# A two-layer transformer on one core: the second attention's stores issued further behind their producers, and its fronts begun twelve steps sooner

## The chip, the cores and the metric

The kernel runs on one core of one Trainium2 chip. The metric is the device time of one execution in microseconds (us). The core has five engines, each with a queue of its own, filled in the order in which the program was written: TensorE (PE, its weight loads shown as PEld), VectorE (DVE), ScalarE (ACT), GpSimd (POOL) and SyncE (SP), whose queue issues most of the DMAs. An instruction that waits for another engine, or for a DMA, holds up what stands behind it in its own queue.

## The reference

`x` is 16 x 512 tokens of 128 numbers, 8192 tokens. Two blocks follow each other, and each adds an attention and a feed-forward network of the normed input to `x`:

```
xn = layernorm(x);  x = x + attn0(xn) + ffn0(xn)     # attn0: 4 layers of mamba, attention, mlp
xn = layernorm(x);  x = x + attn1(xn) + ffn1(xn)
```

The change touches the second block alone. `attn1` has 16 heads of 64. Queries and keys are rotated by position; keys serve as values too. A window of 128 queries sees its own and the previous window's keys, layer-normed, and one key for each 16 tokens that lie wholly before the query:

```
pkv = softmax(gkv @ Wproj)                  # over the 16 tokens of a segment
gkv = layernorm(sum of the 16 tokens, weighted by pkv)
sim = [q @ gkv (masked), q @ layernorm(local keys) (masked)]
out = softmax(sim) @ [gkv, layernorm(local keys)]
attn1 = out (all heads) @ Wout + bout
```

`ffn1` sends each token to the one of 8 experts that has its largest routing probability (at most 1024 tokens an expert), and adds the expert's output times that probability.

## The kernel before, in words

The first block fills some 5650 us and is not touched. The second block is written by a Python scheduler that runs when the program is built: `manual_schedule` keeps the instructions in exactly the order in which the Python code emits them, engine by engine.

The tokens are cut into 64 **units** of 128 (four to a sequence, `TB` = 4, `t` = 0 to 3 within it). Each unit has 16 heads in four **groups** of four heads. The main loop (from L1475) runs over 256 groups, `i` = 4 x unit + group. In a turn it emits

- `scores(i)` (L1327): four matmuls `s` into PSUM; four VectorE operations `am` that add the mask and take the maximum (L1350); four exponentials on ScalarE (L1351); a copy `pg` of the weights of the segment keys;
- `weights_by_key(i - 1, two)` for `two` = 0, 1 (L1359): transposes `gp` and `pp` on TensorE and copies `gt` (VectorE) and `pt` (ScalarE). The PSUM pool of `s`, `gp` and `pp` has five buffers, so `pp` of group i - 1 takes a buffer that `am` of group i has just read;
- `values(i - 2, two)` (L1378): matmuls `o` of the weights with `gvb` (segment keys) and `lk` (local keys), and for every second group a copy `ot` on ScalarE.

Between these the loop calls `work(1)`, six times a turn. `work` is one **cycle** of the rest: Python generators, called streams, each with the number of the cycle at which it may go on. A stream that yields `-n` lets n cycles pass; `+n` does the same and also ends the cycle for the streams after it in the list; 0 asks again in the next cycle. A unit's four turns take 24 cycles. The streams, in order of rank:

- `back(u)` (L1407), put in when the last scores of unit u are written: reciprocal of the sums, transposed into `rd`, `rd` stored to DRAM (L1418) and read back as `rb`, spread over the partitions (L1425); when the unit's values are written (`U.done`), GpSimd multiplies `ot` by `rb` (L1430); four cycles later TensorE's output projection `m_po` (eight matmuls, and `x1`), VectorE's bias addition `ro` (L1437) and, two cycles on, the store `r_d` (L1439).
- `front(u)` (L1157), the keys and queries of unit u: load `xu`; projections `m_kv`, rotated (`by_cos` on VectorE, copy `raw` on ScalarE, `raw`, `kv` on GpSimd); projections `m_q`, their products `q` on VectorE, their sum `qt` on GpSimd (L1208); mean `hm` and difference `hd` (VectorE), `by_w` (GpSimd, L1217), squares `hq` (ScalarE), `hv` and `pl` (VectorE, L1222 and L1234); `hr` and `hw`, the inverse root (ScalarE, GpSimd); transpose `m_plt`; normed keys `n`, segment softmax `se`; transposes `m_nt` into `lkt` (L1261); `lk` (L1271); `sw`, `m_gp`, `gm` to `gv` for the segment keys (`gr` L1296 to L1298, `lk` again L1299, `gv` L1304); `gv` stored to DRAM (L1308), transposed as `m_gkt`, and read back into `gvb` by four loads (L1323). `front(u)` starts only when front u - 1 has written `n` (`normed`).
- `routing()` (L999): the routing of all tokens, then 64 scatters of 128 tokens each to the experts' rows in DRAM (`xts` loaded by SyncE, L1079; indirect DMA on GpSimd, L1081), then the experts, 16 halves of 512 rows (`m_xep`, `m_hp`, `he`, `m_yp`, `ye`).
- `results()` (L1129): when all experts are written, for each tile of 128 tokens a gather `gy` (indirect DMA on GpSimd, L1137), a load `res` of the attention's result (L1144), three cycles, the sum `res` on VectorE (L1146) and at once the store to `out` (L1147).

Buffers that the change is near: `qt` has three, `lk` four (`lks[u % 4]`, read by units u and u + 1), `xts` four, `gv_d`, `rd_d` and the blocks `gvb` two each; the pool behind `misc`, for all PSUM of the streams, two.

The loop calls `begin()` for two fronts ahead of the first turn and then one at the first group of each unit; `while unfinished(i // 4): work(1)` holds the scores of a unit back until its front is written.

Of the kernel before, what the change touches and what calls it, by code (L numbers as in the profile page):

```python
# [23 lines left out]
NT = T // P  # L24
# [45 lines left out]
def tile_kernel(  # L70
# [16 lines left out]
    nc = tc.nc  # L87
# [38 lines left out]
    with (  # L126
# [770 lines left out]
        while done_t[0] < n_cycles or ready or streams or due or deferred:  # L897
            i, at = divmod(done_n[0], PC)
# [19 lines left out]
            if ready and ready[0][0] <= tick[0]:  # L918
                at, k, i = ready.pop(0)
# [3 lines left out]
            if do_t and done_t[0] % 4 == 3:  # L923
                k, t = divmod(done_t[0], 8)
# [14 lines left out]
    with (  # L939
# [59 lines left out]
        def routing():  # L999
# [73 lines left out]
            nc.vector.tensor_copy(slot, sl)  # L1073
            yield -1
            xts = {}
            for t in range(NT + 3):
                if t < NT:
                    xts[t] = wk.tile([P, D], F32, name=f"xts_{t}", tag="xts", bufs=4)
                    nc.sync.dma_start(xts[t], xt_d[t * P : (t + 1) * P, :])  # L1079
                if t >= 3:  # L1080
                    nc.gpsimd.indirect_dma_start(  # L1081
                        out=xe_d,
                        out_offset=bass.IndirectOffsetOnAxis(ap=slot[:, t - 3 : t - 2], axis=0),
                        in_=xts.pop(t - 3),
                        in_offset=None,
                    )
                yield -2
# [41 lines left out]
        def results():  # L1129

            while not experts_done[0]:
                yield 0
            for t in range(NT):
                while stored[0] <= t:
                    yield 0
                gy = wk.tile([P, D], F32, name=f"gy_{t}", tag="gy", bufs=3)
                nc.gpsimd.indirect_dma_start(  # L1137
                    out=gy,
                    out_offset=None,
                    in_=ye_d,  # L1140
                    in_offset=bass.IndirectOffsetOnAxis(ap=slot[:, t : t + 1], axis=0),
                )
                res = wk.tile([P, D], F32, name=f"res_{t}", tag="res", bufs=3)
                nc.sync.dma_start(res, r_d[t * P : (t + 1) * P, :])  # L1144
                yield -3
                nc.vector.scalar_tensor_tensor(res, gy, pk[:, t : t + 1], res, ALU.mult, ALU.add)  # L1146
                nc.sync.dma_start(out[t * P : (t + 1) * P, :], res)  # L1147

        class Unit:
# [7 lines left out]
        def front(u):  # L1157
# [30 lines left out]
            k, c_, s_ = halves(kv), halves(by_cos), halves(raw)  # L1188
            nc.gpsimd.tensor_tensor(k[:, :, 0, :], c_[:, :, 0, :], s_[:, :, 1, :], ALU.subtract)  # L1189
            nc.gpsimd.tensor_tensor(k[:, :, 1, :], c_[:, :, 1, :], s_[:, :, 0, :], ALU.add)  # L1190
            U.qt = wk.tile([P, NHP, P], F32, name=f"qt_{u}", tag="qt", bufs=3)
            for c in range(2):
                parts = []
# [53 lines left out]
            nc.vector.tensor_tensor(se, plv, smx.unsqueeze(2).broadcast_to(shape), ALU.subtract)  # L1247
            nc.scalar.activation(se, se, AF.Exp)
            U.normed = True
            yield 2  # L1250
            ss = wk.tile([H1, n_seg], F32, name=f"ss_{u}", tag="ss")
            nc.vector.tensor_reduce(ss, se, AX.X, ALU.add)
            nc.vector.reciprocal(ss, ss)
# [2 lines left out]
            for c in range(2):  # L1256
                ps = misc(f"nt_{u}_{c}")
                n2 = n.rearrange("p h d -> p (h d)")
                for i in range(4):
                    at = (4 * c + i) * P  # L1260
                    nc.tensor.transpose(ps[:, i * P : (i + 1) * P], n2[:, at : at + P], ident)  # L1261
                nc.scalar.activation(
                    lkts[b % 2][:, 4 * c : 4 * c + 4, t * KW : t * KW + P],
                    ps.rearrange("p (i t) -> p i t", t=P),
                    AF.Identity,
                    scale=g_col,
                    bias=b_col,
                )
                yield 1
            lk = U.lk  # L1270
            nc.gpsimd.tensor_tensor(lk, n, row(1).unsqueeze(1).broadcast_to(heads), ALU.mult)  # L1271
            ps = misc(f"pwp_{u}")
# [32 lines left out]
                gv, gd.unsqueeze(1).broadcast_to([P, 2, DH1]), row(4).unsqueeze(1).broadcast_to([P, 2, DH1]), ALU.add  # L1305
            )
            yield -5
            nc.sync.dma_start(gv_d[u % 2], gv[:, 0, :])  # L1308
            ps = misc(f"gkt_{u}")
            nc.tensor.transpose(ps[:, 0:P], gv.rearrange("p a d -> p (a d)"), ident)  # L1310
            for a in range(2):
# [5 lines left out]
                nc.scalar.copy(to, keys.unsqueeze(2).broadcast_to([64, NHP, n, n_seg]))  # L1317
            yield 1
            yield -2
            src = gv_d[u % 2].rearrange("(g j s) d -> j s g d", j=4, s=n_seg)  # L1320
            for j in range(4):
                at = 32 * j + t * n_seg
# [4 lines left out]
        def scores(i):  # L1327

            u, g = divmod(i, 4)
            U = units[u]  # L1330
            b, t = divmod(u, TB)
            n = NK if t else KW
            at = max(t - 1, 0) * KW
            if g == 0:
                U.done = False
                U.sum = wk.tile([P, H1], F32, name=f"sum_{u}", tag="sum", bufs=2)
            G = groups[i] = Group()
            G.pts = []
            pr = G.pr = wk.tile([P, 4, NK], F32, name=f"pr_{i}", tag="pr", bufs=2)
            pss = []  # L1340
            for j in range(4):
                h = 4 * g + j
                hp, r = h // 2, slice(64 * (h % 2), 64 * (h % 2) + 64)
                s = ps_s.tile([P, S], F32, name=f"s_{i}_{j}", tag="s")
                mm(s[:, 0:n], U.qt[r, hp, :], lkts[b % 2][r, hp, at : at + n])
                pss.append(s)
            for j, s in enumerate(pss):

                nmax = wk.tile([P, 1], F32, name=f"am_{i}_{j}", tag="am", bufs=8)
                nc.vector.tensor_tensor_reduce(pr[:, j, 0:n], s[:, 0:n], mask(t), -1.0, BIG, ALU.add, ALU.min, nmax)  # L1350
                nc.scalar.activation(  # L1351
                    pr[:, j, 0:n], pr[:, j, 0:n], AF.Exp, bias=nmax, scale=-1.0, accum_out=U.sum[:, 4 * g + j : 4 * g + j + 1]
                )
            G.pg = wk.tile([P, 4, NSEG], F32, name=f"pg_{i}", tag="pg", bufs=2)
            nc.scalar.copy(G.pg, pr[:, :, W:KW])
            if g == 3:
                streams.insert(0, [back(u), tick[0] + 2])

# [19 lines left out]
        def values(i, two):  # L1378
# [24 lines left out]
                U.ot = wk.tile([P, NHP, P], F32, name=f"ot_{u}", tag="ot", bufs=2)  # L1403
            nc.scalar.copy(U.ot[:, 2 * g - 2 : 2 * g + 2, :], U.o)
            U.done = g == 3

        def back(u):  # L1407

# [5 lines left out]
            nc.tensor.transpose(ps[0:H1, 0:P], U.sum, ident)  # L1414
            rd = wk.tile([H1, P], F32, name=f"rd_{u}", tag="rd", bufs=2)
            nc.vector.tensor_copy(rd, ps[0:H1, 0:P])
            yield 2
            nc.sync.dma_start(rd_d[u % 2], rd)  # L1418
            x1 = wk.tile([P, P], F32, name=f"x1u_{u}", tag="x1u", bufs=2)
            nc.sync.dma_start(x1, x1_d[b][:, t * P : (t + 1) * P])  # L1420
# [7 lines left out]
            yield -1  # L1428
            units.pop(u)
            nc.gpsimd.tensor_tensor(U.ot, U.ot, rb, ALU.mult)  # L1430
            yield -4
            po = misc(f"po_{u}")
            for i in range(NHP):
                mm(po[:, 0:D], U.ot[:, i, :], wout_sb[:, i, :], i == 0, False)
            mm(po[:, 0:D], x1, ident, False, True)
            res = wk.tile([P, D], F32, name=f"ro_{u}", tag="ro", bufs=2)
            nc.vector.tensor_tensor(res, po[:, 0:D], bout_row, ALU.add)  # L1437
            yield 2
            nc.sync.dma_start(r_d[u * P : (u + 1) * P, :], res)  # L1439
            stored[0] = u + 1  # L1440
            yield -1

        streams = []
        tick = [0]

        def work(n):

# [27 lines left out]
        begin()  # L1475
        NG1 = 4 * NU
        for i in range(NG1 + 2):
            if i % 4 == 0 and begun[0] < NU:
                begin()
            if i < NG1:  # L1480
                while unfinished(i // 4):
                    work(1)
                scores(i)
                work(1)
            for two in range(2):
                if 0 <= i - 1 < NG1:
                    weights_by_key(i - 1, two)
                    work(1)
                if i >= 2:
                    values(i - 2, two)  # L1490
                    work(1)
            work(1)
# [108 lines left out]
```

## Time and profile before

| | us |
|---|---|
| Median of 3 runs (7825.79 to 7835.86) | 7826.6 |
| Profiled execution's own time | 7828.71 |
| Its span | 7826.9 |
| First scores of unit 0 in the span | 5684.5 |
| TensorE busy over the span | 7010.5 (90%) |
| VectorE, ScalarE, GpSimd busy | 4782.5, 4616.3, 3012.6 |
| Mean granted TensorE clock | 0.938 |

In the rows of the profile, a line names the engine, the line of the kernel, the operation, the tile written and the tiles read, and in brackets or behind a bar the idle time ahead of it with the work that ended that idle time. A row of waits gives the waiting engine, line and tile, the releaser, the total, the number of times and the longest. `SPq` is SyncE's queue. Where matmuls go through the helper of the second block, their line is L994, so tiles tell them apart.

### The profile page before, as it was taken

The page shows a single profiled execution, that of the slowest core. Times are in us where ns is not written, and L with a number is a line of the kernel's source. Part 1 is how long each engine was busy: PE and PEld are TensorE (multiplying, and loading weights), DVE is VectorE, ACT ScalarE, POOL GpSimd, SP SyncE. Part 2 cuts the span into 40 slices and gives each one's busy share as a digit, 9 for nine tenths or more (in the row PEclk, how much of TensorE's full clock was granted, in tenths as well). Part 3 has the DMA queues.
Part 4 walks back from the last instruction along what each step waited for, and adds up shares of the span by engine and source line. Part 5 has one row for each costly group of instructions (what it writes and reads, how often), then busy time and mean ns, then how long its engine had stood idle before and what let it go on. Part 6 is the DMA issues. An engine that isn't in the chain of part 4 may idle for free. (4 is left out here: it accounts for less than half of the span.)

```text
span 7826.9 us, 107889 instructions
## 1 busy us (share of the span) xinstructions
PE 7010.5 (90%) x38168; PEld 3230.2 (41%) x38168; DVE 4782.5 (61%) x9622; ACT 4616.3 (59%) x9357; POOL 3012.6 (38%) x3763
## 2 busy tenths in 40 slices
PE   6898999999999999999999999999678999889898
PEld 2233333333333333333333333333256666666666
DVE  4565666566666666666666666666266555666665
ACT  3565655566555666656666666656355666556666
POOL 3333332232323233222222222222268655667775
PEclk7999999999999999999999999999789999989999
DMA  2221222212222221122211222222211111111111
GB/s 70 80 81 66 74 69 66 85 62 68 69 71 69 70 66 65 63 67 70 71 60 62 69 79 71 81 74 88 83 28 52 51 41 46 42 44 34 33 35 36
DMA packets 394780, 492.23 MB, mean 63 GB/s; under 512 B 82304, under 2 KB 278016, under 8 KB 393088
## 3 DMA queue, kind: packets, MB, share of 16 engines
q1 hardware_dynamic: 390144, 476.94, 19.5%
q0 software_dynamic: 4096, 8.40, 0.4%
q8 instruction: 302, 4.95, 0.3%
q14 instruction: 238, 1.95, 0.1%
HBM read 348.87 MB, written 133.17 MB: 62 GB/s over the span
## 5 line engine op out<-in xcount | busy, mean ns | idle before, releaser
L915 DVE TENSOR_REDUCE nm<-n 128x1 f32<-128x512 f32 x4096 | 2587.5, 682 | 1479.6 <-PE n L177 1477.9
L917 ACT ACTIVATE pt<-t 128x512 f32<-128x512 f32 x4096 | 2216.3, 595 | 1882.1 <-PE t L177 1857.4
L177 PE MATMUL n<-kt,qt 72*128 72x512 bf16 x4096 | 1323.5, 389 | 203.5 <-DVE nm L915 158.9
L177 PE MATMUL t<-qt,kt 75*128 75x512 bf16 x4096 | 1357.9, 391 | 104.1 <-ACT pt L917 56.0
L177 PE MATMUL o<-pt,vt 128*32 128x512 f32 x8192 | 1123.0, 671 | 0.0
L177 PEld LDWEIGHTS <-qt 72*128 72x128 bf16 x4096 | 354.7, 98 | 1026.3 <-issue 881.9
L177 PEld LDWEIGHTS <-kt 75*128 75x128 bf16 x4096 | 399.9, 99 | 849.8 <-issue 519.8
L1351 ACT ACTIVATE pr<-pr,am 128x288 f32<-128x288 f32 (+1 forms) x1024 | 508.0, 498 | 209.8 <-DVE am L1350 209.2
L867 POOL CAST nmp<-nm 128x16 bf16<-128x16 f32 x256 | 50.0, 195 | 1451.3 <-DVE nm L915 1451.3
L177 PEld LDWEIGHTS o<-pt,vt 128*32 128x32 f32 x8192 | 231.0, 118 | 661.1 <-issue 526.0
L467 POOL TENSOR_TENSOR qk<-qk,parts 128x512 f32<-128x512 f32 x128 | 147.9, 1155 | 769.3 <-ACT parts L280 739.7
L1350 DVE CUSTOM_DVE_ANT_0 pr<-s,cst 128x288 f32<-128x288 f32 (+1 forms) x1024 | 372.6, 419 | 44.5 <-PE s L994 44.1
L1373 PE MATMUL pp<-ident,pr 128*128 128x128 f32 x1792 | 311.5, 294 | 94.5 <-DVE am L1350 93.6
L994 PE MATMUL o<-pt,lk 128*64 128x128 f32 x3584 | 327.3, 300 | 0.0
L1375 ACT COPY pt<-pp 128x512 f32<-128x512 f32 (+1 forms) x512 | 264.9, 526 | 97.4 <-PE pp L1373 95.8
L1200 DVE TENSOR_TENSOR q<-m_q,cst 128x512 f32<-128x512 f32 x256 | 177.1, 692 | 220.1 <-PE m_q L994 220.1
L994 PE MATMUL s<-lkt,qt 64*128 64x288 f32 (+1 forms) x2048 | 298.3, 408 | 0.4 <-ACT lkt L1317 0.4
L177 PE MATMUL m_in<-x,w 128*128 128x512 f32 x512 | 279.6, 632 | 17.9 <-POOL x L330 9.7
L1373 PEld LDWEIGHTS pp<-ident,pr 128*128 128x128 f32 x1792 | 214.8, 148 | 162.9 <-DVE am L1350 130.2
L994 PE MATMUL m_q<-xu,wq_sb 128*128 128x128 f32 x2048 | 278.5, 279 | 1.9 <-ACT raw L1183 0.8
L177 PE MATMUL m_f<-n,w 128*128 128x512 f32 x512 | 274.0, 618 | 2.9 <-POOL n L330 2.6
L994 PEld LDWEIGHTS m_q<-xu,wq_sb 128*128 128x128 f32 x2048 | 249.4, 192 | 20.1 <-ACT raw L1183 16.0
(333 smaller groups left out, 11104.7 us busy)
## 6 DMA issues: line engine op xcount, KB each, us to landing
qt<-q_d SPq DMA_DIRECT2D x768, 96.0 KB
kt<-k_d SPq DMA_DIRECT2D x256, 288.0 KB
rb_n<-rstd_d SPq DMA_DIRECT2D x64, 512.0 KB
rb<-rd SPq DMA_DIRECT2D x128, 256.0 KB
q_d<-parts SPq DMA_DIRECT2D x64, 384.0 KB
k_d<-parts SPq DMA_DIRECT2D x64, 384.0 KB
o_d<-og SPq DMA_DIRECT2D x512, 36.0 KB
oa<-o_d SPq DMA_DIRECT2D x64, 256.0 KB
```

Source lines behind the costliest of these rows:

```text
L177: nc.tensor.matmul(out, lhsT=lhsT, rhs=rhs, start=first, stop=last)
L467: nc.gpsimd.tensor_tensor(x, x, parts[:, 0], ALU.subtract)
L867: nc.gpsimd.tensor_copy(parts[:, 0], nm)
L915: nc.vector.tensor_reduce(dst, n, AX.X, ALU.max, negate=True)
L917: nc.scalar.activation(dst, n, AF.Exp)
L994: nc.tensor.matmul(out, lhsT=lhsT, rhs=rhs, start=first, stop=last)
L1200: nc.vector.tensor_tensor(q, ps.rearrange("p (i t) -> p i t", t=P), const(name)[:, t * P : (t + 1) * P].unsqueeze(1).broadcast_to([P, 4, P ...
L1350: nc.vector.tensor_tensor_reduce(pr[:, j, 0:n], s[:, 0:n], mask(t), -1.0, BIG, ALU.add, ALU.min, nmax)
L1351: nc.scalar.activation(pr[:, j, 0:n], pr[:, j, 0:n], AF.Exp, bias=nmax, scale=-1.0, accum_out=U.sum[:, 4 * g + j : 4 * g + j + 1])
L1373: nc.tensor.transpose(pp[:, a, c, :], G.pr[:, 2 * two + a, at : at + P], ident)
L1375: nc.scalar.copy(pt[:, :, 0:n, :], pp[:, :, 0:n, :])
```

## The change

Nothing is computed differently. The order in which instructions are written, and so the order in each queue, changes:

- `routing()`: the scatter of a tile is written two steps behind its load, no longer three.
- `results()`: four cycles pass between the sum `res` and its store to `out`.
- `front(u)`: two guards, `while scored[0] < u - 2` ahead of `qt` and `while valued[0] < u - 2` ahead of `lk`; `normed` is followed by three cycles, no longer two; the store of `gv` moves from ahead of `m_gkt` to three cycles behind it, and four cycles pass before the `gvb` loads.
- `back(u)`: `rd` is stored five cycles behind its copy (two before); `m_po` follows `ot` by six cycles (four before); `r_d` is stored five cycles behind `ro` (two before).
- `scored` counts the units whose last scores are written (set at the end of `scores`), `valued` those whose last values are (at the end of `values`).
- The main loop begins a front at the third group of a unit, twelve cycles sooner than at the first group of the next, and a third one at the very start.

```diff
-            for t in range(NT + 3):
+            for t in range(NT + 2):
...
-                if t >= 3:
+                if t >= 2:
                     nc.gpsimd.indirect_dma_start(
                         out=xe_d,
-                        out_offset=bass.IndirectOffsetOnAxis(ap=slot[:, t - 3 : t - 2], axis=0),
-                        in_=xts.pop(t - 3),
+                        out_offset=bass.IndirectOffsetOnAxis(ap=slot[:, t - 2 : t - 1], axis=0),
+                        in_=xts.pop(t - 2),
...
                 nc.vector.scalar_tensor_tensor(res, gy, pk[:, t : t + 1], res, ALU.mult, ALU.add)
+                yield -4
                 nc.sync.dma_start(out[t * P : (t + 1) * P, :], res)
...
             nc.gpsimd.tensor_tensor(k[:, :, 1, :], c_[:, :, 1, :], s_[:, :, 0, :], ALU.add)
+            while scored[0] < u - 2:
+                yield 0
             U.qt = wk.tile([P, NHP, P], F32, name=f"qt_{u}", tag="qt", bufs=3)
...
             U.normed = True
-            yield 2
+            yield 3
...
+            while valued[0] < u - 2:
+                yield 0
             lk = U.lk
...
             yield -5
-            nc.sync.dma_start(gv_d[u % 2], gv[:, 0, :])
             ps = misc(f"gkt_{u}")
...
             yield 1
             yield -2
+            nc.sync.dma_start(gv_d[u % 2], gv[:, 0, :])
+            yield -4
             src = gv_d[u % 2].rearrange("(g j s) d -> j s g d", j=4, s=n_seg)
...
+            scored[0] += g == 3
...
+            valued[0] += U.done
...
             nc.vector.tensor_copy(rd, ps[0:H1, 0:P])
-            yield 2
+            yield 5
             nc.sync.dma_start(rd_d[u % 2], rd)
...
             nc.gpsimd.tensor_tensor(U.ot, U.ot, rb, ALU.mult)
-            yield -4
+            yield -6
             po = misc(f"po_{u}")
...
             nc.vector.tensor_tensor(res, po[:, 0:D], bout_row, ALU.add)
-            yield 2
+            yield 5
             nc.sync.dma_start(r_d[u * P : (u + 1) * P, :], res)
...
+        scored, valued = [0], [0]
...
-            if i % 4 == 0 and begun[0] < NU:
+            if (i == 0 or i % 4 == 2) and begun[0] < NU:
                 begin()
```

## The prediction

> **What bounds the kernel now.** I read the table of stretches first, to see what the second attention costs, then who waits on TensorE there, then one unit's rows on TensorE, VectorE and GpSimd, last the stalls of SyncE's queue. I call one step of the written schedule a cycle; a unit has 24. The stage's units start where the `s` rows start (eight matmul rows a group, four groups a unit).
>
> ```profile
> 5804.20:6136.30 332.10, 279.35 (x2349) 207.53 (x2348) 204.18 (x591) 196.39 (x585) 270.72 (x253) 0.94 0.19 52
> 6136.30:6680.80 544.50, 513.73 (x4187) 375.47 (x4186) 311.16 (x900) 335.10 (x945) 309.22 (x285) 0.99 0.17 44
> 6680.80:7040.40 359.60, 293.52 (x2353) 219.98 (x2352) 221.28 (x630) 193.47 (x582) 237.95 (x227) 0.89 0.17 44
> 7040.40:7706.30 665.90, 598.27 (x5175) 448.64 (x5174) 445.11 (x1321) 428.07 (x1278) 477.63 (x440) 0.96 0.13 34
> ```
>
> Columns: stretch, length, busy us of PE, PEld, DVE, ACT, POOL, granted clock. These are units 3–12 (scatter beside them), 13–27 (experts), 28–37 (results caught up), 38–59 (nothing beside them): 33.2, 36.3, 36.0 and 30.3 us a unit. TensorE is busy 84 to 94%: its idle time and its clock are what can be won. Who makes it wait, from unit 0 on:
>
> ```profile
> PE pp L1373 <- DVE am L1350: 93.6, 48, 6.8
> PE m_po L994 <- POOL ot L1430: 66.7, 56, 3.8
> PE o L994 <- DMA gvb<-gv: 33.3, 8, 5.2
> PE m_nt L1261 <- DVE se L1247: 28.1, 23, 1.4
> ```
>
> The change aims at the last three. The first is the largest. A `pp` transpose of group i-1 needs the PSUM buffer that `am` of group i empties, so VectorE must reach `am` of a group soon after TensorE has made its scores, or TensorE stops. One late unit shows it:
>
> ```profile
> 7449.78 1.24 PE L994 MATMUL s<-lkt,qt 64*128 64x288 f32 x8
> 7453.83 2.05 PE L994 MATMUL m_po<-wout_sb,ot 128*128 128x128 f32 x16 [0.69 <-POOL ot L1430]
> 7456.85 1.24 PE L994 MATMUL s<-lkt,qt 64*128 64x288 f32 x8
> 7459.99 0.66 PE L1373 MATMUL pp<-ident,pr 128*128 128x128 f32 x4 [1.64 <-DVE am L1350]
> ```
>
> ```profile
> 7452.28 1.21 DVE L1211 TENSOR_REDUCE hm<-kv 128x16 f32<-128x1024 f32 x1
> 7453.53 1.33 DVE L1213 SCALAR_TENSOR_TENSOR hd<-hm,kv 128x1024 f32<-128x1024 f32 x1
> 7456.14 0.29 DVE L1437 TENSOR_TENSOR ro<-m_po,rows_sb 128x128 f32<-128x128 f32 x1 [1.28 <-PE m_po L994]
> 7456.35 1.21 DVE L1222 TENSOR_REDUCE hv<-hq 128x16 f32<-128x1024 f32 x1
> 7458.34 1.22 DVE L1234 TENSOR_REDUCE pl<-by_w 128x16 f32<-128x1024 f32 x1 [0.78 <-POOL by_w L1217]
> 7459.48 0.45 DVE L1350 CUSTOM_DVE_ANT_0 pr<-s,cst 128x288 f32<-128x288 f32 x1
> ```
>
> From the third group's scores to the released `pp` pass 10.2 us (7449.78 to 7459.99), and VectorE's norm chain sets them: `hm`, `hd`, ACT's `hq`, `hv`, `pl`. The 0.69 before `m_po` lies inside these 10.2 us, so it costs nothing there. In units 28–37 another wait decides:
>
> ```profile
> 6766.63 0.33 SPq L1308 DMA_DIRECT2D gv<-gv  x1
> 6776.17 0.34 SPq L1147 DMA_DIRECT2D out<-res  x1
> 6776.55 0.43 SPq L1144 DMA_DIRECT2D res<-r_d  x1
> 6777.10 1.34 SPq L1323 DMA_DIRECT2D gvb<-gv  x4
> ```
>
> ```profile
> 6779.03 0.76 PE L994 MATMUL o<-gt,gvb 128*128 128x128 f32 x2 [5.09 <-DMA gvb<-gv]
> ```
>
> SyncE's queue stands 9.5 us at the `out` store, behind a VectorE result, with the `gvb` loads queued after it.
>
> **The change part by part.** Line numbers are before's.
>
> Stores (`out` L1147, `r_d` L1439, `gv` L1308, `rd` L1418) leave SyncE's queue free. The four `gvb` loads then wait only for the values that read the old block. Issued most of a group ahead of the values that read the new block, they land in time: the 32.1 us of `gvb` waits in units 28–37, and the lower clock (0.89 against 0.96), go. `r_d` later by three cycles delays only `res`, which no engine but VectorE's `res` row waits for. `gv` later by three cycles lets `gvb` follow it by four. The later `rd` leaves some 6 cycles, about 7 us, for `rb` before `ot`; hidden behind two groups of values, and without that cover it would cost what the one `rb` wait of the trace cost, 13.2 us on GpSimd. As `out` now takes 7 cycles a tile instead of 3, results catch up at two a unit, and take units 31–59 instead of 28–37: GpSimd's `gy` gather (1.09 us) and VectorE's `res` (0.33) come twice in each.
>
> Scatter lag 3 to 2 (L1076): SyncE's 186.8 us of waits before `xts` loads shrink; TensorE waited for none of it. Cost 0; with its cover (loads four cycles ahead) gone, at most one landing a tile. The two guards (`scored`, `valued`): in the written order neither ever holds a front back. But GpSimd now writes `qt` and `lk` only 5 and 4 cycles (1.28 us each) behind TensorE's last reads of those buffers, before 15 and 14. TensorE needs under 2 us for such reads, and GpSimd stands idle 2.8 us ahead of `gr` anyway: cost 0, and some 2 us of GpSimd a unit if the cover is gone, ahead of `raw`, which is in the bounds below.
>
> `ot` to `m_po` two cycles wider: the 66.7 us go nearly everywhere, but only where that wait is not inside VectorE's chain does time go. `m_nt` one cycle wider: 12.1 us over 22 late units, 0.55 a unit, go.
>
> Fronts twelve steps sooner, with `po` later, change who shares a group, and this is the term that decides. Before, the norm chain shares its group with `m_po`. After, the written order of TensorE's heavy group is `s, gkt, gp, pp, q, o, pp, o, s`; `m_po` sits two groups later, beside `nt` and `gp`. VectorE's order is four `am`, `gt`, the last `q`, `hm`, `hd`, `hv`, `pl`, `res`, then the next `am`; GpSimd's is `qt, gy, by_w`, with `ot` gone from among them. From that group's scores: `am` starts at 0.8 and the four take 1.5; `q` ends on TensorE at 2.9, on VectorE at 3.6; `hm` 1.25, `hd` 1.35, `hq` 1.15, `hv` 1.2: 8.6. GpSimd: `gr` now stands behind four `am`, so `gv` ends and `raw` starts 2.2 us later after its group's scores than before (6.6 for 4.4), that is 2.1 before the heavy scores; `raw` 2.4, `kv` 2.4, `qt` 1.25 bring 4.0; the second `qt` 1.25 to 2.25, `gy` 1.25, `by_w` 2.35: 8.8 to 9.8. So `pl` starts there, ends at 10.0 to 11.0, `res` 0.3, `am` to `pp` 0.5: 10.8 to 11.9. Without `gy` and `res` 10.6. I take 11.4, nearest to the row of the second `qt`, which took 2.26 in every late unit beside `hd`: +1.2 (bounds +0.4, +1.7).
>
> The same shift moves 2.1 us of `m_po` (7453.83 to 7455.94) out of the stretch that VectorE sets, and a `q` (1.0) and `gkt` (0.2) into it: 1.0 us of TensorE work that was free must be paid elsewhere (+1.0; bounds +0.8, +1.1). `q`'s first product waits for the `raw` copy, now behind four exponentials: +0.4 (0, +0.7). TensorE's stop grows from 1.64 to about 5 us. After 1.64 us the second `pp` ran 1.06 instead of 0.66, after 5.09 `m_po` took 3.62 instead of 2.05. The granted clock over this late unit is 0.94, 3.7 us at half speed, 1.8 lost; over the 39.9 us of the unit with the 5.09 it is 0.87, 10.4 us at half, of which the stop itself covers some. One half-speed stretch more, partly under the stop: +0.7 (0, +1.7). With `m_nt` -0.5 (bounds -1.4, 0): **+2.8 us a late unit**, 33.1 us.
>
> [...]
>
> The sum, stretch by stretch:
> - units 38–59: 22 x 2.8 = +62, and +6 for two of the last four.
> - units 28–37: 36.0 to 33.1, -29.
> - experts, 13–27: the expert matmuls now fill the heavy group (5.1 us of its own, 3.3 of experts), so TensorE needs there what VectorE's chain needs without `gy`. `m_po` 14.7 and `m_plt` 9.3 us of waits go, `raw` and a small `pp` wait come: -0.7 x 15 = -10 (-1.9 to +1.0 each).
> - units 3–12: a scatter (1.02 us) stands where `gy` does, 33.1 for 33.2: 0 (-1.9 to +2.3 each).
> - start and tail: more of front 1 ahead of the first scores, +4 (-10, +15).
>
> Together +33. The profiled execution took 7828.7 us (span 7826.9), the median of the runs is 7826.6, 2.1 less. 7828.7 + 33 - 2.1 = 7860 us.
>
> **The rivals.**
> *Faster:* the chain ends no later than today (`by_w` in time, no `raw` wait, the same clock window). Then +1.2 a unit: 24 x 1.2 = 29, catch-up -45, scatter -17, experts -10, ends +4: -39, 7788 us. For it: `ot` leaves GpSimd's chain; against it: `gr` and `gy`. It decides below +2.1 a unit (44 units break even at 32.4 us).
> *Much slower:* the second `qt` is held through `hd` and `gy` follows late, two half-clock windows each unit: +4.2, 24 x 4.2 = 101, -15, +13, -5, +10: +104, 7930 us.
> *No effect:* SyncE's stops were mostly hidden (424.9 us at `r_d`, 418.0 at `gv`, and TensorE lost 33 by them), and gain and loss cancel: 7826 us.
>
> **How the numbers follow.** Forecast 0.50 (7832 to 7892), faster rival 0.25, much slower 0.15, no effect 0.10. A measurement tells 0.2%, 16 us. Faster 0.25; same 0.15 (no effect, and the forecast's low edge); slower 0.60. The range runs from the faster rival to short of the dearest case: 7785 to 7915.
>
> **What would show it.** Right: no `gvb` waits; `m_po` waits on `ot` near nothing; `pp` on `am` several times 93.6 us, 4 to 5 us in each late unit, in the group where `hm`, `hd`, `hv`, `pl` stand; late units near 33 us, with `gy` and `res` up to unit 59; the clock there below 0.96. Wrong: late units at 31.5 or less, which would say that `pl` did not wait for `by_w`; or units 3–27 moving by more than 2 us each, which I put near nothing.

## The result, and the profile after

The changed kernel took 7968.77 us (median of 4 runs, 7961.75 to 7975.87) against 7826.19 (4 runs, 7813.34 to 7835.86): ratio 1.0178, 95% interval 1.0165 to 1.0191. The forecast was 7860, so the sign was right and the size was not: 143 us instead of 33. The profiled executions took 7965.63 and 7828.71 us (spans 7963.8 and 7826.9), and they show where the time went. Stretches run from the first `s` row of a unit to that of another.

| stretch | before, us | after, us | difference | predicted |
|---|---|---|---|---|
| up to the first scores, and units 0-2 | 5804.2 | 5812.6 | +8.4 | +4 with the tail |
| units 3-12, scatters | 332.1 | 368.7 | +36.6 | 0 |
| units 13-27, experts | 544.5 | 578.1 | +33.6 | -10 |
| units 28-37 | 359.6 | 346.3 | -13.3 | -29 |
| units 38-59, the late units | 665.9 | 733.8 | +67.9 | +62 |
| units 60-63 and tail | 120.6 | 124.3 | +3.7 | +6 for two of the units |

The table of stretches of the changed kernel (columns as before: stretch, length, busy us of PE, PEld, DVE, ACT, POOL, clock, share of DMA, GB/s):

```profile
5812.60:6181.30 368.70, 290.95 (x2372) 223.26 (x2364) 207.66 (x598) 196.36 (x584) 273.55 (x251) 0.87 0.15 42
6181.30:6759.40 578.10, 512.43 (x4105) 385.82 (x4104) 311.47 (x898) 332.53 (x937) 317.09 (x293) 0.94 0.16 42
6759.40:7105.70 346.30, 289.69 (x2443) 222.51 (x2442) 210.03 (x608) 201.14 (x593) 221.96 (x206) 0.91 0.15 38
7105.70:7839.50 733.80, 592.68 (x5173) 458.54 (x5172) 461.38 (x1341) 431.61 (x1276) 498.50 (x462) 0.90 0.14 37
```

TensorE is busy as long as before over these four (1685.8 us against 1684.9), so the time added there is time in which it stands; and its clock is lower in three of the four (0.87 for 0.94, 0.94 for 0.99, 0.90 for 0.96). Who made it wait, from unit 0 on:

```profile
PE pp L1380 <- DVE am L1356: 232.1, 48, 9.4
PE m_xep L1110 <- DMA xe<-xe_d: 42.6, 15, 3.9
PE m_pwp L1278 <- ACT lkt L1265: 39.9, 41, 1.1
PE m_pwp L1278 <- POOL se L1257: 24.6, 9, 4.5
...
PE m_po L994 <- POOL ot L1438: 4.7, 1, 4.7
...
PE o L994 <- DMA gvb<-gv: 3.6, 2, 2.3
```

The change does what it says: `m_po` waits for `ot` once instead of 56 times, `gvb` costs 3.6 us instead of 33.3, the wait of `m_nt` is gone but for 0.8 us. But `pp` waits 232.1 us instead of 93.6, and two waits have come up: `m_xep` for the experts' rows (none before), `m_pwp` for `lkt` (39.9 us, 1.3 before). In a late unit, the heavy group's scores, and then the `pp` behind the next scores:

```profile
7238.85 1.24 PE L994 MATMUL s<-lkt,qt 64*128 64x288 f32 x8
```

```profile
7243.93 1.24 PE L994 MATMUL s<-lkt,qt 64*128 64x288 f32 x8
...
7250.41 1.12 PE L1380 MATMUL pp<-ident,pr 128*128 128x128 f32 x4 [4.98 <-DVE am L1356]
```

VectorE's and GpSimd's rows between them:

```profile
7242.43 1.21 DVE L1214 TENSOR_REDUCE hm<-kv 128x16 f32<-128x1024 f32 x1
7243.68 1.45 DVE L1216 SCALAR_TENSOR_TENSOR hd<-hm,kv 128x1024 f32<-128x1024 f32 x1
7246.25 1.22 DVE L1225 TENSOR_REDUCE hv<-hq 128x16 f32<-128x1024 f32 x1 [1.12 <-ACT hq L1222]
7248.50 1.22 DVE L1237 TENSOR_REDUCE pl<-by_w 128x16 f32<-128x1024 f32 x1 [1.03 <-POOL by_w L1220]
7249.63 0.34 DVE L1146 SCALAR_TENSOR_TENSOR res<-gy,pk,res 128x128 f32<-128x128 f32 x1
7249.89 0.45 DVE L1356 CUSTOM_DVE_ANT_0 pr<-s,cst 128x288 f32<-128x288 f32 x1
```

```profile
7241.53 2.51 POOL L1211 TENSOR_TENSOR qt<-q,q 128x512 f32<-128x512 f32 x2
7244.20 1.88 POOL L1137 DMA_INDIRECT gy<-ye_d,slot  x1 [0.16 <-issue]
7246.12 2.34 POOL L1220 TENSOR_TENSOR by_w<-kv,rows_sb 128x1024 f32<-128x1024 f32 x1
```

From scores to `pp` pass 11.56 us (7238.85 to 7250.41; the prediction had 11.4), TensorE stops for 4.98 (predicted about 5), and `pl` waits for `by_w`, behind `qt` and `gy`, as predicted.

### The profile page after: what moved, and what is told of

Same layout as the page of the kernel before. It is cut to its first block, busy times and chain, and to the rows that moved or that the text cites. A ratio compares the mean times of both kernels' runs of the same rounds, so it can differ in the third digit from the quotient of the medians.

```text
span 7963.8 us, 107766 instructions
## 1 busy us (share of the span) xinstructions
PE 7011.7 (88%) x38168; PEld 3268.2 (41%) x38168; DVE 4797.0 (60%) x9622; ACT 4622.9 (58%) x9357; POOL 3024.5 (38%) x3763
## 5 line engine op out<-in xcount | busy, mean ns | idle before, releaser
L1380 PE MATMUL pp<-ident,pr 128*128 128x128 f32 x1792 | 334.5, 310 | 232.1 <-DVE am L1356 232.1
L994 PEld LDWEIGHTS m_q<-xu,wq_sb 128*128 128x128 f32 x2048 | 248.4, 192 | 20.0 <-ACT raw L1184 11.7
```

Of the source, the lines that this page charges most:

```text
L994: nc.tensor.matmul(out, lhsT=lhsT, rhs=rhs, start=first, stop=last)
L1380: nc.tensor.transpose(pp[:, a, c, :], G.pr[:, 2 * two + a, at : at + P], ident)
```

## The experiments

All runs in us per unit (profiled execution), with the ratio to the kernel before, measured beside it, and its 95% interval. The profiled executions of e8 and e9 (7845.2 and 7945.5 us) lie 13 and 14 us under the medians of their runs, the others within 8 us of theirs:

| run | ratio | units 3-12 | 13-27 | 28-37 | 38-59 |
|---|---|---|---|---|---|
| before | 1 | 33.2 | 36.3 | 36.0 | 30.3 |
| after | 1.0178 (1.0165-1.0191) | 36.9 | 38.5 | 34.6 | 33.4 |
| e1 front alone | 1.0114 (1.0093-1.0135) | 37.1 | 35.2 | 35.3 | 33.4 |
| e2 all but front | 1.0042 (1.0027-1.0056) | 32.3 | 40.9 | 32.5 | 31.0 |
| e3 after, lag 3 | 1.0156 (1.0136-1.0177) | 38.2 | 35.3 | 34.3 | 34.6 |
| e4 after, `hv` and `pl` later | 1.0404 (1.0386-1.0421) | 39.6 | 44.7 | 35.9 | 35.2 |
| e5 after, `xe` ahead | 1.0100 (1.0081-1.0119) | 37.1 | 35.4 | 33.9 | 33.4 |
| e6 after, no scatters | 1.0101 (1.0077-1.0125) | 33.4 | 37.9 | 34.6 | 33.4 |
| e7 before, no scatters | 0.9950 (0.9937-0.9964) | 30.2 | 36.4 | 35.8 | 30.2 |
| e8 all but front, lag 3 | 1.0027 (1.0015-1.0039) | 34.6 | 38.7 | 31.9 | 30.9 |
| e9 after, short reductions | 1.0158 (1.0122-1.0193) | 37.1 | 38.0 | 34.2 | 33.4 |
| e10 before, short reductions | 0.9952 (0.9938-0.9967) | 35.5 | 35.4 | 35.6 | 29.1 |
| e11 before, lag 2 | 0.9976 (0.9963-0.9989) | 33.9 | 34.9 | 35.8 | 30.3 |
| e12 later stores alone | 1.0060 (1.0038-1.0083) | 35.9 | 35.4 | 33.0 | 33.3 |
| e13 after, `by_w` ahead | 1.0210 (1.0193-1.0227) | 38.6 | 38.3 | 35.1 | 34.2 |
| e14 e13 and e9 | 1.0198 (1.0180-1.0217) | 38.9 | 38.0 | 34.9 | 34.2 |
| e15 lag 2, `gv` later | 1.0021 (1.0011-1.0031) | 36.5 | 35.7 | 35.2 | 30.6 |
| e16 lag 2, other stores later | 1.0028 (1.0016-1.0039) | 34.3 | 35.0 | 33.7 | 33.1 |
| e17 e14 and e18 | 1.0067 (1.0047-1.0088) | 38.8 | 38.1 | 32.6 | 30.9 |
| e18 after, `res` free | 1.0170 (1.0149-1.0192) | 36.8 | 38.4 | 34.2 | 33.4 |

### Which part: front or spacings (e1, e2)

e1 makes of the kernel before (and puts in the two guards, which hold nothing back in the written order):

```diff
-            if i % 4 == 0 and begun[0] < NU:
+            if (i == 0 or i % 4 == 2) and begun[0] < NU:
```

> The kernel before with the earlier beginning of the fronts alone (and the two counters that guard it); stores, projection, normed keys and scatters stand as before. Theory (the earlier front puts VectorE's norm chain hm, hd, hq, hv, pl of the next unit beside the group that has no projection, so that pp waits for am there, and puts scatters and ye copies in the way of a front's work): the loss is nearly all of it here too, 7940 us, between 7910 and 7990; units 38 to 59 at 33 us each or more, pp waiting 4 us or more per late unit for am; units 3 to 12 above 36 us. Rival (the wider spacings cost the time, the front is neutral): within 20 us of before, 7806 to 7846, late units at 30.3 us, units 3 to 12 at 33 us.

e2 undoes this line in the kernel after.

> The kernel after with the fronts begun where the kernel before begins them; the later stores, the wider spacings and the scatters' lag of two stay. Theory (the front does the harm, the store delays help a little): at or below before, 7785 us, between 7765 and 7830; late units 30.3 us, units 28 to 37 at 32 to 34 us instead of 36, units 3 to 12 at 33 us, pp waiting 2 us or less per late unit for am. Rival (the spacings cost the time): 7900 to 7970, late units at 32 us or more. Rival for the scatter phase alone (the lag of two costs it): units 3 to 12 stay near 36.9 us.

e1 took 7920.14 us (+91), inside its range: the front brings the loss of the scatter units and of the late units whole. But the expert units gain, and the late units lose by other waits, 33.35 us all the same:

```profile
PE gp L1371 <- ACT pt L1380: 55.0, 19, 3.8
PE pp L1378 <- DVE am L1354: 44.7, 21, 2.4
PE o L994 <- DMA gvb<-gv: 13.1, 10, 3.7
```

There ScalarE's queue carries the wait: `pt` stands behind `hq`, which waits for `hd`, and `gp` needs `pt`. e2 missed: 7862.27 us, slower than before. Scatter units, units 28 to 37 and late units were near what was expected (32.3, 32.5, 31.0 us), the expert units were not (40.9). So the front alone is a loss, and so is all the rest without it; the expert units gain in e1 (35.2) and lose in e2.

### The expert units (e3, e5, e11, e8)

In the changed kernel's expert units the new wait is that of `m_xep`. SyncE's queue and TensorE there:

```profile
6424.86 0.39 SPq L1127 DMA_DIRECT2D ye_d<-ye  x1
6425.29 0.51 SPq L1106 DMA_DIRECT2D xe<-xe_d  x1
```

```profile
6428.97 0.63 PE L1110 MATMUL m_xep<-ident,xe 128*128 128x128 f32 x4 [2.01 <-DMA xe<-xe_d]
```

The store of one half's `ye` waits for VectorE, and the next half's `xe` load is behind it: it goes out 3.7 us ahead of the transposes that need it. e5 puts the next half's load just ahead of that store, every step in its place:

```diff
             yield 2
+            if 2 * e + hf < 2 * E - 1:
+                expert_half.xe[2 * e + hf + 1] = load_xe(2 * e + hf + 1)
             nc.sync.dma_start(ye_d[at : at + S, :].rearrange("(t p) d -> p t d", p=P), ye)
```

> The kernel after with the next half's xe load issued just ahead of this half's ye store instead of behind it; every step keeps its place. Theory (in the expert units xep waits because SP holds the xe load behind a ye store that waits for VectorE's ye copy, and the load stands only three cycles ahead of xep): xep's 2 to 4 us per expert unit vanish, units 13 to 27 at 36 us or less instead of 38.5, total 7925 to 7940 us. Rival (the half's other waits, for lkt and pt on ScalarE, take the time over): units 13 to 27 at 38 us, total 7955 to 7975 us.

```profile
6184.10:6715.10 531.00, 490.59 (x4105) 369.34 (x4104) 309.58 (x898) 331.16 (x937) 317.30 (x293) 0.98 0.17 45
```

7912.74 us. Units 13 to 27 take 531.0 us instead of 578.1, no wait of `m_xep` is left among them, and the clock is back to 0.98. That is 47 us for waits that sum to 36.5 us there, and not all of these come back: TensorE's idle time falls by 25 us (65.7 to 40.4), as `m_pwp` now waits longer for `lkt` (14.3 us for 4.8), and its busy time by 22, with the higher clock. Without the wait of `m_xep` the expert units are 13.5 us under before, where the prediction had -10.

e3 gives the changed kernel the old lag (`NT + 3`, `t >= 3`):

> The kernel after with the scatters' lag of three steps as before, all else as after. Theory (scatters cost time because they stand between a front's POOL steps, not because their tile comes late): the same as after, 7958 to 7978 us, units 3 to 12 at 36 to 37 us. Rival (the lag of two makes the scatters wait for their loads and POOL with them): 7930 to 7945 us, units 3 to 12 back at 33 to 34 us.

7953.28 us, just under the range of its theory, which was right about the scatters (38.2 us, no gain) and right in the total by chance: the expert units fell by 49 us, as in e5, and the late units rose by 28, for which no run here isolates the cause. In the written order, the lag sets at which cycles of a unit the halves fall: in the changed kernel `xe` is loaded three cycles ahead of `m_xep`, in e3 five. A half takes one unit in each, and keeps its cycles through all 16. e11 makes the lag alone two in the kernel before (the first lines of the change's diff):

> The kernel before with the scatters' lag of two steps instead of three and nothing else. Theory (the lag does nothing to the scatters, and moves the expert halves to other steps): units 3 to 12 within 0.5 us of 33.2, late units at 30.3 us; units 13 to 27 change by more than 1 us per unit, in either direction, and carry all of the difference. Rival (the lag matters to the scatters alone): units 13 to 27 within 0.5 us of 36.3 and units 3 to 12 change by 1 us or more.

```profile
6154.20:6678.40 524.20, 502.77 (x4187) 371.58 (x4186) 312.65 (x900) 334.01 (x945) 309.77 (x285) 1.00 0.18 46
```

7820.11 us beside 7839.09: the expert units go from 544.5 to 524.2 us at a clock of 1.00, the scatter units lose 7 us, where the theory had none, and the late units stay. Of the versions that leave nothing out it alone is faster than the kernel before, by 0.2%. e8, which gives e2 the old lag, was to bring the expert units back too:

> The later stores and wider spacings with fronts and scatters as in the kernel before: the lag of three steps moves the expert halves to other steps than in the run without the earlier front and with the lag of two, where units 13 to 27 took 40.9 us. Theory (the expert units' time is set by which steps a half falls on, not by the spacings): units 13 to 27 at 35 to 37 us, late units at 31 us as in that run, total 7785 to 7815 us. Rival (the spacings themselves cost the expert units): units 13 to 27 at 40 us or more, total 7850 to 7870 us.

It did not, or not far enough: 7858.62 us, expert units at 38.7 us for 40.9, now with `m_yp` waiting for `he` (40.8 us); in e2 it was `m_hp` for `xeT` (75.8 us over 15 units). So the lag alone, which moves the halves and changes no work, is worth 1.4 us a unit in the kernel before, 3.2 in the kernel after and 2.2 in e2, not always the same way, and the leading wait changes with it (`m_po` to `m_hp`, `m_xep` to `m_pwp`, `m_hp` to `m_yp`).

### The scatter units (e6, e7)

Both replace a tile's load and scatter by one copy from memory to memory (shown for the kernel after):

```diff
-                if t < NT:
-                    xts[t] = wk.tile([P, D], F32, name=f"xts_{t}", tag="xts", bufs=4)
-                    nc.sync.dma_start(xts[t], xt_d[t * P : (t + 1) * P, :])
                 if t >= 2:
-                    nc.gpsimd.indirect_dma_start(
...
+                    nc.sync.dma_start(xe_d[(t - 2) * P : (t - 1) * P, :], xt_d[(t - 2) * P : (t - 1) * P, :])
```

> The kernel after with each xts load and its scatter on POOL replaced by one unsorted copy of the same 64 KB from memory to memory on SP's queue at the scatter's step; the rows are not put in the experts' order, which this kernel leaves out. Theory A (the scatter units lose what the late units lose, the scatters add the same few us as in the kernel before): units 3 to 12 at 33.3 to 34 us, that is 3 us below after, as much as the same edit takes from the kernel before. Theory B (the earlier front makes the scatters dearer, since they now stand between by_w, ot and se on POOL): more than 5 us per unit are gained here, and 3 us or less in the kernel before.

> The same edit in the kernel before (rows not put in the experts' order). Theory A (scatters cost the same few us in both): units 3 to 12 at 30.3 us, its late units' time, 2.9 us below before, total 7790 to 7805 us. Theory B (scatters cost little in the kernel before): units 3 to 12 at 32 to 33 us, total 7810 to 7830 us.

Units 3 to 12 of e6:

```profile
5803.50:6137.40 333.90, 281.12 (x2374) 215.38 (x2366) 211.09 (x598) 195.39 (x584) 212.66 (x196) 0.90 0.14 36
```

and of e7:

```profile
5809.00:6111.20 302.20, 270.34 (x2348) 201.41 (x2347) 199.36 (x591) 195.28 (x585) 206.19 (x190) 0.97 0.17 44
```

Scatters cost 34.8 us over the ten units in the kernel after (55 of them) and 29.9 before (63). So of the +36.6, 31.7 (333.9 less 302.2) is there without a scatter, and only 4.9 is scatters made dearer; theory A carries six sevenths of it. On average the 31.7 is the late units' loss of 3.1 us a unit, but it does not fall evenly: without scatters units 3 to 7 lose 4.6 us each and units 8 to 12 only 1.7, though in the latter `pp` waits for `am` nearly as in a late unit (4.5 us a unit). The scatters' price moves the other way (units 3 to 7: 1.8 us a unit against 2.8; units 8 to 12: 5.2 against 3.2). That the early front makes the loss is shown (37.1 us in e1, 32.3 in e2); which wait makes it in units 3 to 7 is not.

### What holds am in a late unit (e4, e9, e10, e13, e14, e17, e18)

e4 moves `hv` and `pl` behind the next scores (`yield -4` for `yield -2` ahead of `hv`):

> The kernel after with four steps instead of two between hq and hv, so that hv and pl fall behind the next group's scores. Theory (the length of VectorE's chain ahead of am in that one group is what pp waits for): pp waits 2 us or less per late unit instead of 5 to 6, late units at 31.5 us instead of 33.3, total 7905 to 7930 us. Rival (am is late since by_w and gy stand late on their engines, or the wait only moves on with hv and pl): late units stay at 33 us or more, total 7955 to 7985 us.

8148.94 us, the worst of all. The wait that it aimed at did go (11.7 us over the late units for 118.6); others came:

```profile
PE m_po L994 <- POOL ot L1438: 74.4, 22, 4.3
PE o L994 <- DMA gvb<-gv: 26.4, 16, 2.0
PE pp L1380 <- DVE am L1356: 11.7, 12, 1.1
```

e9 and e10 shorten the reductions and move nothing (shown for `hm`; `hv`, `pl` likewise):

```diff
-            nc.vector.tensor_reduce(mean, kv, AX.X, ALU.add)
+            nc.vector.tensor_reduce(mean, kv[:, :, 0:4], AX.X, ALU.add)
```

> The kernel after with the three reductions of the front's norm chain on VectorE (hm, hv and pl) taken over 4 elements of each head instead of 64: the steps, the order and every other instruction stay, and the means, variances and scores that they feed are left wrong. Theory (what pp waits for in the late units is the length of this chain on VectorE in a group that has little work on TensorE): the chain is some 3.3 us shorter (three reductions of 1.21 us), pp's wait falls from 5 to 6 us to about 2, late units to 30.5 us or less, units 3 to 12 to 34 us, total 7870 us or less. Rival (am is late since by_w comes late from POOL or hq from ScalarE): late units at 32.5 to 33.4 us, total above 7930 us.

> The same edit in the kernel before. Theory (the chain lies beside the projection's matmuls there and is nearly covered): pp's wait of 1.6 us per late unit goes and no more, late units at 28.7 to 29.5 us, 1 to 1.5 us under before, against 2.8 us or more in the kernel after. Rival (the chain costs as much in both): late units at 27.5 us or less.

In the kernel before it takes 1.1 us from a late unit; in the kernel after, where VectorE's busy time in the late units fell by 73 us (461.38 to 388.83), nothing (33.36). The theory that the length of VectorE's chain alone holds `am` fell. e13 issues `by_w` right behind `kv`, e14 does both:

> The kernel after with by_w's multiplication on POOL issued right behind kv, ahead of q and of both qt and gy; nothing else moves. Theory (two chains of nearly one length hold am in the late units: POOL's qt, qt, gy, by_w up to pl, and VectorE's hm, hd, hv with hq on ScalarE): pl no longer waits, the 1.0 us gap ahead of it goes and pp's wait falls by about 1 us, late units at 32 to 32.7 us, total 7920 to 7950 us. Rival (by_w alone holds am): late units at 31 us or less, total below 7900 us.

> The same with the three reductions hm, hv and pl over 4 of 64 elements of each head (the means, variances and scores that they feed are left wrong). Theory of two chains: with both shortened am comes 3 us or more sooner, pp's wait falls to 2 us or less, late units at 30.5 us or less, total 7885 us or less. Rival (a third thing holds am, as the group's place among the scores): late units at 32.5 us or more.

Both slower, 34.2 us a late unit, and both theories missed; the third thing of e14's rival is there. VectorE's rows of e14 name the third thing:

```profile
7256.50 0.21 DVE L1237 TENSOR_REDUCE pl<-by_w 128x16 f32<-128x64 f32 x1
7260.36 0.35 DVE L1146 SCALAR_TENSOR_TENSOR res<-gy,pk,res 128x128 f32<-128x128 f32 x1 [3.66 <-DMA gy<-ye_d,slot]
```

`pl` ends 3 us sooner, and VectorE stands at `res`, the results' row in front of `am`, until the gather has landed; with `by_w` ahead, GpSimd issues the gather later, 8.0 us behind the start of the first `am` instead of 4.6. e18 computes `res` from a constant row, e17 does all three:

```diff
-                nc.vector.scalar_tensor_tensor(res, gy, pk[:, t : t + 1], res, ALU.mult, ALU.add)
+                res = wk.tile([P, D], F32, name=f"rf_{t}", tag="xts", bufs=4)
+                nc.vector.scalar_tensor_tensor(res, bout_row, pk[:, t : t + 1], bout_row, ALU.mult, ALU.add)
```

> The kernel after with the results' res computed from a constant row alone (result rows left wrong), by_w and the reductions as in after. Theory (the landing of gy is one of three, and not the last in this order): late units within 0.5 us of 33.35, total 7950 to 7980 us. Rival (the landing of gy alone holds am): late units at 32 us or less, total below 7940 us.

> The kernel after with by_w ahead, the three reductions over 4 of 64 elements, and the results' res computed from a constant row instead of the gathered gy and the loaded r_d, which are still gathered and loaded (norms, scores and the result rows are left wrong). Theory (three things end within about 1 us of each other ahead of am: VectorE's chain, POOL's by_w, the landing of gy; each alone hides behind the others): pp's wait falls to 2.5 us or less, late units at 31 us or less instead of 33.35, units 28 to 37 at 33.5 us or less, total 7900 us or less. Rival (something else holds am or takes the wait over): late units at 32.8 us or more.

e18 changes nothing (33.36 us). e17 brings 2.4 us: late units at 30.9, near before's 30.3. Its `pp` still waits 3.0 us a unit, where 2.5 or less was expected. TensorE's first wait in e17's late units, 118.6 us in the kernel after:

```profile
PE pp L1381 <- DVE am L1357: 66.3, 22, 3.8
```

So three things end within a microsecond of each other ahead of `am` in the unit shown above: `hv` at 7247.47, the landing of `gy` at 7247.74, `by_w` at 7248.46. No single cure gains anything, and all three together do; of the pairs only `by_w` ahead with short reductions was run (e14).

That a single cure gains nothing has a second reason, which the traces show in TensorE's clock. In e9 the cure does reach TensorE: `pp` waits 101.5 us in the late units instead of 118.6, and TensorE's idle time there falls by 19 us (141.1 to 122.0). Its busy time rises by as much (592.68 to 611.90 us):

```profile
PE pp L1380 <- DVE am L1356: 101.5, 22, 5.4
```

```profile
7086.90:7820.80 733.90, 611.90 (x5173) 471.72 (x5172) 388.83 (x1341) 431.76 (x1276) 504.83 (x462) 0.90 0.14 37
```

Around one stop, the two stretches at half clock, in the kernel after and then in e9:

```profile
7247.78:7251.19 3.41, 0.78 (x4) 0.79 (x5) 2.69 (x9) 1.05 (x5) 2.92 (x7) 0.50 0.07 19
7251.19:7254.61 3.42, 3.42 (x19) 2.57 (x17) 1.91 (x5) 2.69 (x9) 0.05 (x1) 0.50 0.27 62
```

```profile
7230.19:7233.60 3.41, 2.71 (x15) 2.16 (x16) 3.11 (x12) 2.70 (x10) 1.96 (x5) 0.50 0.28 76
7233.60:7237.02 3.42, 3.42 (x19) 2.65 (x20) 0.56 (x2) 1.75 (x4) 0.09 (x1) 0.50 0.01 4
```

Over the 22 late units the clock is halved for 150.2 us in both kernels, 6.83 us (twice 3.41) a unit, whether the stop shown is 4.98 us long or 4.26; what the shorter stop brings is taken by more work at half clock (4.1 us a unit in the kernel after, 6.0 in e9). Of the 205 half-clock stretches in the trace of the kernel after, and of the 186 in that of the kernel before, all but the last of each are whole multiples of 3.41 us. And four late units, one sequence, take, from unit 40 on, 133.1 us in the kernel after, 133.0 to 133.2 in e5, e6, e9 and e18, and 136.5 to 136.7 in e13 and e14: 39 and 40 times 3.413, a step of 0.85 us a unit. The kernel before (120.5 to 121.6) and e17 (121.3 to 124.6) keep to no such step. So a cure of less than a step need not show in the time here, and that e9 and e18 gain nothing does not tell how much of the time the other two things hold. Why the loop falls in with these steps no run tests.

There is a further tie between the chains in e9: with `hm` short, `hd` falls beside the second `qt`, and the two `qt` take 3.5 us instead of 2.5, so that `by_w` ends no sooner.

### Which of the stores (e12, e15, e16)

e12 is the kernel before with all later stores and nothing else; e15 has the lag of two and `gv`'s alone; e16 the lag of two and all but `gv`'s.

> The kernel before with the later stores alone (gv, rd, r_d and out issued two to four steps further behind); fronts, projection, normed keys and scatters as before. Theory (the stores let SP go past the waits that hold gvb in units 28 to 37, and the wider spacing of the normed keys is what makes late units 31 us without the earlier front): late units at 30.3 us, units 28 to 37 at 31.5 to 32.5 us, units 13 to 27 between 35 and 41 us by where the halves fall, total 7775 to 7830 us. Rival (later stores cost the late units): late units at 31 us.

> The kernel before with the lag of two and gv's store and loads issued later, and no other change. Theory (the four steps that gv's loads stand later are what let the next unit's front run up to three steps sooner against the scores in the run of the stores alone): late units at 33 us or more, pp waiting 3.5 us or more for am. Rival (rd's or r_d's store does it): late units at 30.3 us.

> The kernel before with the lag of two and the stores of rd, r_d and out issued later, gv's left where it was. Theory (these three leave fronts and expert halves where they are, and the store of out let past is what ends the waits for gvb in units 28 to 37): units 13 to 27 at 34.9 us, late units at 30.3 to 31 us, units 28 to 37 at 32 to 34 us instead of 35.8, total 7780 to 7805 us, faster than both. Rival (gvb is held by gv's own early store): units 28 to 37 at 35.5 us or more, total 7815 to 7835 us.

All three missed the total or the late units. The later stores do take the waits for `gvb` out of units 28 to 37 (33.0 and 33.7 us a unit for 36.0; in e15, where `out`, `rd` and `r_d` are not delayed, 25.4 us of these waits stay and the units take 35.2), but e12 and e16 give it back in the late units: units 28 to 59 took 1025 us before, 1063 and 1064 here. There the results pass at two tiles a unit until unit 53 or 54, where before they were done with the backlog by unit 37. With `m_po` and the normed keys spaced wider besides, e2 and e8 take 1008 and 1000. `gv`'s store alone is not it (30.6). Whether `out`'s delay or those of `rd` and `r_d` cost the late units was not separated.

## Why the prediction was wrong

**The late units: right, in part by luck.** +2.8 a unit was the term, +3.09 measured. The path it was built on (`qt`, `gy`, `by_w`, `pl`, `res`, `am`: 11.4 us) measured 11.56, the stop 4.98. It had the end of `hv` at 8.6 us behind the scores and that of `by_w` at 8.8 to 9.8; they came at 8.62 and 9.61. But 11.4 was taken for a second `qt` of 2.26 us beside `hd`, and here `hd` waited instead: the two `qt` took 2.51 us together, and the gather 1.88 where 1.25 stood in the sum. Two errors made up for each other. What it left out is the landing of the gather, 8.89 us behind the scores, for which `res` waits; that matters to whoever mends it. Of the other parts, no wait for `raw` shows on TensorE, and a new wait of 1.0 for `lkt` does. The clock term of +0.7 fits: the clock is halved for 6.83 us a late unit instead of 2.64 (44 times 3.41 us over the 22 units instead of 17 times), and of that TensorE works 4.1 us instead of 2.6, by which an estimate of 0.7 more is lost (half of the difference). Nor is the early front the only way there: the later stores alone bring the late units to 33.3 us (e12).

**"Units 3-12: a scatter (1.02 us) stands where `gy` does, 33.1 for 33.2: 0": the step that failed first.** The 33.1 was a late unit with its two gathers, and one scatter was put in their place; before, 63 scatters come in these ten units, 6.3 each. e7 shows that they cost 3.0 us a unit, so a unit without them is 30.2, and the front's loss had to be added to all of 33.2. It came out as 31.7 us, and 4.9 for dearer scatters. The trace of before held the hint: 33.2 against 30.3 is the price of scatters, and the sum replaced it instead of keeping it.

**"Experts: -0.7 x 15 = -10": a term left out.** e5 shows -13.5 without the new wait of `m_xep`, which takes 47 us. The sum placed the halves' matmuls but left out their DMAs: it did not ask where the `xe` load falls, behind which store, and how many cycles ahead of `m_xep`. The lag, costed at 0, decides it: it moves every half to other cycles. In units 13 to 27 the lag of two is worth +49 us in the kernel after (e3) and -20 in the kernel before (e11), on the same line. The -10 itself rests on a unit without `gy` and `res` at 10.6 us; its own terms (8.6, 1.2 and 0.5) add up to 10.3.

**Units 28-37: -13 for -29.** Units 31 to 37 took 33.2 us each, as predicted; units 28 to 30 still held expert halves and took 114.0 us instead of 99. In the changed order five or six scatters pass in a unit instead of seven, so the halves end in unit 30 and not in 28; the sum kept the stages where they were.

**The rest.** The guards and `m_po` did as said, and the stores did in units 28 to 37; alone they cost the late units 3 us each (e12), for which the sum had no term of its own. Two readings were loose, and neither moved the sum: TensorE was busy 82% of units 28 to 37, not 84 or more, and in the kernel before `pl` already waited 0.78 us for `by_w`, so VectorE's chain alone did not set the 10.2 us. The much slower rival (+104) came nearer in total, by a late unit of +4.2 that did not happen, though its two half-clock windows a unit did (the 44 stretches of 3.41 us above); no rival had the scatter or the expert units as its source. The sign named as "wrong", units 3 to 27 moving by more than 2 us each, is what happened.

## What to carry to other kernels

In an order written out by hand, a step moved in one stage moves whatever is paced beside it in the next: price the loss in every stage in which the moved work runs, on top of what that stage already pays, and follow the loads of the side streams too, by how far ahead of their first reader they are issued and behind which wait. Where several chains end together ahead of one instruction, curing one can show nothing (e9, e13, e18): read the row in front of the waiting instruction after each cure, and take them away together before calling a chain innocent. And read idle time and clock apart: in these late units a shorter stop was paid back in slower work (e9: 19 us less idle time, 19 us more busy time).

## What the runs showed of the hardware that was not expected

In the late units `hd`, a VectorE operation with two inputs of 128 x 1024, ends 1.1 us behind the end of a GpSimd product, however early it was started. In e1, GpSimd's and VectorE's rows:

```profile
7226.09 2.36 POOL L1219 TENSOR_TENSOR by_w<-kv,rows_sb 128x1024 f32<-128x1024 f32 x1
```

```profile
7226.41 3.14 DVE L1215 SCALAR_TENSOR_TENSOR hd<-hm,kv 128x1024 f32<-128x1024 f32 x1
```

`by_w` ends at 7228.45 and `hd` 1.10 later, at 7229.55. In all 154 late units of seven of the kernels (before, after, e1, e4, e12, e15, e16) `hd` ends 1.08 to 1.10 us behind a product of GpSimd, so it took from 1.27 to 3.75 us by what stood there. A product that GpSimd begins during `hd` is itself some 1.0 us longer (the second `qt` of 2.26 us in the prediction; `by_w` 3.35 in e12), except in five units of e1, where a gather ran as `hd` began and `by_w` went first at its usual 2.35. This is also how e1 comes to its late units: `by_w` stands earlier there, `hd` waits it out, and `hq`, `pt` and `gp` behind it. In these units, then, `hd` loses the rest of one whole product of the other engine, and not a share of its rate; by what the two engines hold each other up no run shows.
